# A graph network on one core: bfloat16 parts in attention's block products, and no counting of sources

## The chip, the core and the metric

The kernel runs on one core of one Trainium2 chip. A core has five engines with instruction streams of their own: PE (TensorE: matrix products; loading its weights is shown as PEld), DVE (VectorE), ACT (ScalarE), POOL (GpSimd) and SP (SyncE). They share the on-chip memory SBUF; products land in PSUM[...], which PE, DVE and ACT can reach. DMA queues, fed by SP, ACT and POOL, move data between SBUF and the chip's main memory. The metric is the device time of one execution in microseconds (us).

## The reference

There are 6,250 nodes with 128 features, 200,000 edges (source, destination, 16 attributes), the edges sorted by destination. Two blocks are added to the residual stream `x`:

```python
h = jnp.maximum(_layernorm(x, axis=-1), 0.0)
x = x + _L0_gnn_ref(h, edge_index, edge_attr_16, ...)     # five attention layers
h = jnp.maximum(_layernorm(x, axis=-1), 0.0)
x = x + _L1_gnn_ref(h, src, dst, theta_w, ...)            # edge convolution
```

An attention layer computes, for every edge and every self loop, a score, a softmax over the edges of one destination, and the weighted sum of the source rows:

```python
h = x @ W
s = leaky_relu((h @ a_src)[src] + (h @ a_dst)[dst] + (ea @ We) @ a_edge, 0.2)
ex = jnp.exp(s - segment_max(s, dst)[dst])
out = segment_sum(h[src] * (ex / denom[dst])[:, None], dst) + b
```

The edge convolution makes a row for each edge, normalizes each feature over all edges, multiplies, normalizes again and takes the mean over the edges of a destination:

```python
e = (h[dst] - h[src]) @ theta_w.T + h[src] @ phi_w.T
e = relu(_bn(e, bn0_g, bn0_b))      # mean and variance over the edges
e = relu(_bn(e @ fc1_w.T, bn1_g, bn1_b))
x = relu(segment_sum(e, dst) / maximum(count, 1) + h)
```

## The kernel before

**Tiling.** Nodes lie in 49 tiles of 128 (`NB`). The edges of a destination are cut into rows of K = 4 edges, padded; 128 such rows make a block, and four blocks (`GQ`) a group, so a group has 16 x 128 edge places. A loop `over` (L125) is written out for 109 groups; further groups for other inputs stand behind an `If` that this input doesn't enter. All rows of a block belong to one node tile. `neq` and `eqt` are the 0/1 matrices of a block (row by node of the tile) and are loaded from main memory group by group, in bfloat16.

**Stages, in order.**
1. *Sort and rows.* The degree of each destination is counted (`count`, L187): for 16 edges per partition at a time DVE makes two 0/1 arrays (L196, L198), and PE multiplies and adds them up (L200). From the degrees come the positions of the rows; POOL fetches the edge records (L480) and DVE makes the lists of indices `srci`.
2. *Five attention layers* (`attention`, L565). `heads` (L544) computes the node rows with their two scores and writes them to a table in main memory. Then come the groups, in `some` (L590). POOL issues 16 indirect DMAs (L594), each of which fetches 128 rows of the table into `g`; `g` has four buffers. DVE adds the scores (`t`, L605), finds each row's maximum and spreads it over the block (`z`, L611), PE transposes (L614), DVE takes the maximum and the running maximum (L615 to L629) and PE returns it to the rows (L636). After the exponential (L644), ACT makes the first of four weighted source rows (`yp`, L650), DVE adds the other three (L653), which gives `y`, 129 columns per row (features and a one for the denominator). ACT makes the 0/1 matrix `oh` in float32 (L656), PE adds the rows of each node, `op` = `oh` times `y` (L660), and DVE adds `op` into `hb` (L663), whose place for a block is read into a register.
3. Between layers: division, bias, a mix with the first layer's result and a small product, then the next `heads`.
4. *Edge convolution.* Node products `A` (for the destination) and `Bt` (for the source) are made; the mean over all edges is a product of the degrees with `A` and `Bt` (L771, L772) and is subtracted from `Bt`, so the sum of squares gives the variance. `A` is kept as three bfloat16 arrays whose sum is the float32 value (`A3`). The **first pass** (L790) gathers `Bt` rows, 16 indirect DMAs a group (L794), lets PE spread `A` over the rows (L804, three bfloat16 products per block, added in PSUM), adds the two (L808), transposes (L811), copies to `xs` (L812), sums squares on ACT (L814), and writes `xs` out. The second and third passes read these back and need no gather.

**Counting of sources.** The mean needs to know how often each node is a source, `outdeg`. It is counted in the attention layers, a fifth of the edges in each: `count` is a generator, and every fifth group asks for its next step (L665). In the compiled order many of these steps stand near the layer's start.

**Order.** Every engine works its own list in a fixed order; the framework draws it up from the program and adds the waits. It mixes operations of neighbouring groups: in attention, `t` of a group is placed ahead of L653 of the group two before it.

Of the kernel before, what the change touches and what calls it, by code (L numbers as in the profile page):

```python
# [9 lines left out]
F32 = mybir.dt.float32  # L10
BF = mybir.dt.bfloat16
I32 = mybir.dt.int32
AF = mybir.ActivationFunctionType
OP = mybir.AluOpType
AX = mybir.AxisListType
# [5 lines left out]
P = 128  # L21
K = 4
G = 16
GQ = G // K
# [7 lines left out]
def gnn_kernel(ctx: ExitStack, tc: tile.TileContext, x, src, dst, ea, Ws, Wes, a_srcs, a_dsts, a_edges,  # L32
# [8 lines left out]
    nc = tc.nc  # L41
    N, D = x.shape
# [49 lines left out]
    more = const.tile([1, 1], I32, name="more")  # L92
    outdeg = const.tile([P, NB], F32, name="outdeg")
    aeloop = const.tile([P, NB, L], F32, name="aeloop")
# [72 lines left out]
    with tc.tile_pool(name="gat", bufs=1) as gp:  # L167
# [14 lines left out]

        slo = gp.tile([P, CE], BF, name="slo")
        shi = gp.tile([P, CE], BF, name="shi")
        posb, vos, tb128, padq = adE, t0E, TS[:, 1:], R6[:, :, 0]

        def count(to, lo, hi, sw, pp, c0=0, c1=CE):  # L187

            po = pp.tile([P, 2, P], F32, name="po", bufs=1)

            io, po = po[:, 0, :], po[:, 1, :NB]
            nc.vector.tensor_copy(io, iota)
            for c in range(c0, c1, G):
                n = min(G, c1 - c)
                ol = sw.tile([P, G, P], BF, name="ol", bufs=2)
                nc.vector.tensor_tensor(ol[:, :n], mid_bc(io, n, P), last_bc(lo[:, c:c + n], n, P), OP.is_equal)  # L196
                oo = sw.tile([P, G, NB], BF, name="oo", bufs=2)
                nc.vector.tensor_tensor(oo[:, :n], mid_bc(io[:, :NB], n, NB), last_bc(hi[:, c:c + n], n, NB), OP.is_equal)  # L198
                for j in range(n):
                    nc.tensor.matmul(po, ol[:, j, :], oo[:, j, :], start=(c + j == c0), stop=(c + j == c1 - 1))  # L200
                yield
            nc.vector.tensor_tensor(to, to, po, OP.add)

# [18 lines left out]
        with tc.tile_pool(name="sort", bufs=1) as sp, tc.tile_pool(name="sortw", bufs=2) as sw, \  # L222
# [82 lines left out]
            halves(dsti, dlo, dhi)  # L305
            nc.vector.memset(deg, 0.0)
            nc.vector.memset(outdeg, 0.0)
            for _ in count(deg, dlo, dhi, sw, pp):
                pass
            halves(srcu, slo, shi)  # L310

# [253 lines left out]
        def attention(l):  # L565
# [20 lines left out]

            with tc.tile_pool(name="edg", bufs=2) as ep, tc.tile_pool(name="edgp", bufs=2, space=PSUM) as pp:
                steps = count(outdeg, slo, shi, ep, pp, CE * l // L, CE * (l + 1) // L)

                def some(q0, n):  # L590
# [54 lines left out]

                    y = ep.tile([P, GQ, D + 1], F32, name="y")
                    for h in range(0, GQ, 2):
                        yp = pp.tile([P, 2, D + 1], F32, name="yp", bufs=2)
                        for j in (h, h + 1):
                            nc.scalar.activation(yp[:, j - h, :], g[:, K * j, :D + 1], AF.Identity, bias=zeroc, scale=ex[:, j, 0:1])  # L650
                        for j in (h, h + 1):
                            for k in range(1, K):
                                nc.vector.scalar_tensor_tensor(y[:, j, :] if k == K - 1 else yp[:, j - h, :], g[:, K * j + k, :D + 1], ex[:, j, k:k + 1],  # L653
                                                               yp[:, j - h, :], op0=OP.mult, op1=OP.add)
                    oh = ep.tile([P, GQ, P], F32, name="oh")
                    nc.scalar.activation(oh, neq, AF.Identity, bias=onec, scale=-1.0)  # L656
                    for h in range(0, GQ, 2):
                        op = pp.tile([P, 2, D + 1], F32, name="op", bufs=2)
                        for j in (h, h + 1):
                            nc.tensor.matmul(op[:, j - h, :], oh[:, j, :], y[:, j, :], start=True, stop=True)  # L660
                        for j in (h, h + 1):
                            a = hbf[:, ds(r[j], D + 1)]
                            nc.vector.scalar_tensor_tensor(a, a, cor[:, j:j + 1], op[:, j - h, :], op0=OP.mult, op1=OP.add)  # L663

                    if q0 % (5 * GQ) == 0 and q0 < QM:  # L665
                        next(steps, None)

                over(GQ, some, lambda: nc.scalar.dma_start(ael[:, K * QM:], ae_d[l, :, K * QM:]))
                for _ in steps:
                    pass  # L670

# [61 lines left out]
    with tc.tile_pool(name="ec", bufs=1) as gp:  # L733
# [10 lines left out]
        nc.vector.memset(sc, 0.0)  # L744
        S0, SC0, S1, PAD, MU1, V1, SC1, SH1, T0, T1 = (sc[:, k:k + 1] for k in range(10))

        with tc.tile_pool(name="ecn", bufs=1) as lp, tc.tile_pool(name="ecp", bufs=2, space=PSUM) as pp:
# [13 lines left out]
            for t in range(0, NB, 2):  # L761
# [5 lines left out]
                nc.vector.tensor_copy(Bt[:, t:t + n, :], ps[:, :n, 1, :])  # L767

            mp = pp.tile([P, D], F32, name="mp", bufs=1)
            for t in range(NB):  # L770
                nc.tensor.matmul(mp, deg[:, t:t + 1].to_broadcast([P, P]), A[:, t, :], start=(t == 0), stop=False)  # L771
                nc.tensor.matmul(mp, outdeg[:, t:t + 1].to_broadcast([P, P]), Bt[:, t, :], start=False, stop=(t == NB - 1))  # L772
            mu = lp.tile([P, D], F32, name="mu")
# [11 lines left out]

        st0 = gp.tile([P, Q], F32, name="st0")
        with tc.tile_pool(name="p1", bufs=2) as ep, tc.tile_pool(name="p1p", bufs=4, space=PSUM) as pp:
            nc.vector.memset(st0, 0.0)

            def some(q0, n):  # L790
                c0 = K * q0
                g = ep.tile([P, G, D], F32, name="g1", bufs=4)
                for j in range(G):
                    nc.gpsimd.indirect_dma_start(  # L794
                        out=g[:, j, :], out_offset=None, in_=btable,
                        in_offset=bass.IndirectOffsetOnAxis(ap=srci[:, c0 + j:c0 + j + 1], axis=0))
                r = regs(3, q0, GQ, PE, (NB - 1) * 3 * P)
                eqt = ep.tile([P, GQ, P], BF, name="eqt1", bufs=4)
                nc.sync.dma_start(eqt, eqt_d[q0 // GQ])

                ar = pp.tile([P, GQ, D], F32, name="ar", bufs=2)
                for j in range(GQ):
                    for k in range(3):
                        nc.tensor.matmul(ar[:, j, :], eqt[:, j, :], A3f[:, ds(r[j] + k * D, D)], start=(k == 0), stop=(k == 2))  # L804
                xs = ep.tile([P, G, P], F32, name="xs", bufs=3)
                for j in range(GQ):
                    xe = ep.tile([P, K, D], F32, name="xe", bufs=4)
                    nc.vector.tensor_tensor(xe, g[:, K * j:K * j + K, :], mid_bc(ar[:, j, :], K, D), OP.add)  # L808
                    ps = pp.tile([P, K, P], F32, name="xps")
                    for k in range(K):  # L810
                        nc.tensor.transpose(ps[:, k, :], xe[:, k, :], ident)  # L811
                    nc.vector.tensor_copy(xs[:, K * j:K * j + K, :], ps)  # L812
                    sq = ep.tile([P, K, P], F32, name="sq")
                    nc.scalar.activation(sq, ps, AF.Square, accum_out=st0[:, q0 + j:q0 + j + 1])  # L814
                nc.sync.dma_start(e0_d[c0 // G], xs.rearrange("p a b -> p (a b)"))

            over(GQ, some)
        nc.vector.tensor_reduce(S0, st0, AX.X, OP.add)

# [5 lines left out]

        scale_of(SC0, S0, bn[:, 0:1])
        npad = float(C * P - E)


        with tc.tile_pool(name="p2", bufs=3) as ep, tc.tile_pool(name="p2p", bufs=4, space=PSUM) as pp:  # L830
            nc.vector.tensor_scalar(T1, bn[:, 1:2], 0.0, None, op0=OP.max)
            ps = pp.tile([P, 1], F32, name="padp", bufs=1)
# [8 lines left out]
            def some(q0, n):  # L841
                i = q0 // GQ
                xs = ep.tile([P, G * P], F32, name="x2")
                nc.sync.dma_start(xs, e0_d[i])
                nc.scalar.activation(xs, xs, AF.Relu, bias=bn[:, 1:2], scale=SC0)
                for q in range(G // 4):
                    ps = pp.tile([P, 512], F32, name="eps")
                    nc.tensor.matmul(ps, fT, xs[:, q * 512:(q + 1) * 512], start=True, stop=True)
                    k = (i * (G // 4) + q) * 2
                    nc.vector.bn_stats(st[:, k:k + 2, :].rearrange("p a b -> p (a b)"), ps)  # L850
# [38 lines left out]
        with tc.tile_pool(name="p4", bufs=3) as ep, tc.tile_pool(name="p4p", bufs=4, space=PSUM) as pp:  # L889
            def some(q0, n):  # L890
# [5 lines left out]
                nc.sync.dma_start(neq, neq_d[i])  # L896
                nc.scalar.activation(es, es, AF.Relu, bias=bn[:, 1:2], scale=SC0)
                oh = ep.tile([P, GQ, P], F32, name="oh4", bufs=2)
# [76 lines left out]
```

## Time and profile before

| | us |
|---|---|
| median of 3 runs (16198.5 to 16206.34) | 16200.36 |
| the profiled execution | 18742.08 |
| its span, first to last instruction | 18740.2 |
| first row gather of attention | 1379.1 |
| last gather of attention | 14792.8 |
| gathers of the first pass | 15025.6 to 17620.5 |

The profiled execution took longer than the timed runs, so its durations of single operations are of use, and its total isn't the total of the runs. In the tables "busy" is the time in which an engine worked, and "idle before" is the time for which it stood ahead of operations of a group, with what ended it. The mean granted TensorE clock was 0.537 of full speed.

In 40 slices of the span, busy tenths of three engines:

```profile
DVE  6433333334333343333343333433333422222378
ACT  0110111111111111111111111111111101111267
POOL 0555666646666646666646666556666356666300
```

The five layers and the first pass can be seen in POOL's row as the stretch from the third slice to the thirty-eighth, with a lower slice where a layer ends.

### The profile page before, as it was taken

Reading aid. Unit: us, or ns where it says so; the run is one execution under the profiler, and the core shown is the slowest. Engines: PE = TensorE matmul, PEld = TensorE weight load, DVE = VectorE, ACT = ScalarE, POOL = GpSimd, SP = SyncE. Lnnn points to the kernel's source line nnn. Section 1 sums busy time; section 2 is a strip of 40 time slices with the busy share of each in tenths; the row PEclk is TensorE's granted clock in tenths of the full one; section 3 lists DMA queues with packets and bytes.
Section 4 is the critical chain, followed back from the end, with each engine's and each line's share of the span. In section 5 each row is a group of like instructions: output and inputs, shape, how many; then the busy total and the mean of one; then the engine's idle time right before and its main releaser. Section 6 shows DMA issues by size and latency. Waiting matters only on the chain. (4 is left out here: it accounts for less than half of the span.)

```text
span 18740.2 us, 108293 instructions
## 1 busy us (share of the span) xinstructions
PE 4383.7 (23%) x24113; PEld 3257.3 (17%) x24113; DVE 7280.4 (39%) x23779; ACT 2812.4 (15%) x5544; POOL 10364.1 (55%) x10984
## 2 busy tenths in 40 slices
PE   4111111111111121111121111211111212222498
PEld 3111111111111111111111111111111111111268
DVE  6433333334333343333343333433333422222378
ACT  0110111111111111111111111111111101111267
POOL 0555666646666646666646666556666356666300
PEclk6555555555555555555555555555555555555699
DMA  3122222232222222222222222222222223333475
GB/s 100 41 60 50 57 55 57 58 60 54 57 57 56 57 55 57 58 57 58 56 55 57 57 57 56 56 57 57 57 58 56 62 87 93 95 95 92 145 254 201
DMA packets 717079, 1361.81 MB, mean 73 GB/s; under 512 B 223808, under 2 KB 486880, under 8 KB 673632
## 3 DMA queue, kind: packets, MB, share of 16 engines
q0 software_dynamic: 348800, 702.54, 18.3%
q1 hardware_dynamic: 338828, 616.20, 10.1%
q10 hardware_dynamic: 28756, 35.62, 0.6%
q8 instruction: 213, 3.49, 0.1%
q14 instruction: 482, 3.95, 0.1%
HBM read 1144.99 MB, written 208.56 MB: 72 GB/s over the span
## 5 line engine op out<-in xcount | busy, mean ns | idle before, releaser
L594 POOL DMA_INDIRECT g<-table,srci x8720 | 8229.2, 944 | 5241.1 <-issue 4659.1
L660 PE MATMUL op<-y,oh 128*128 128x129 f32 x4360 | 1455.5, 473 | 4624.1 <-DVE y L653 3021.3
L794 POOL DMA_INDIRECT g<-btable,srci x1744 | 1645.8, 944 | 1181.9 <-issue 512.7
L660 PEld LDWEIGHTS op<-y,oh 128*128 128x128 f32 x4360 | 1043.0, 318 | 5086.6 <-issue 3637.1
L653 DVE SCALAR_TENSOR_TENSOR yp<-g,ex,yp 128x129 f32<-128x129 f32 x4360 | 1331.7, 352 | 1393.6 <-DVE yp L653 735.5
L656 ACT ACTIVATE oh<-neq,onesq 128x512 f32<-128x512 bf16 x545 | 392.7, 721 | 5499.8 <-PE op L660 4182.0
L614 PE MATMUL xp<-ident,z 128*128 128x128 f32 x2180 | 607.4, 434 | 2482.5 <-issue 724.1
L663 DVE SCALAR_TENSOR_TENSOR hb<-hb,cor,op 128x129 f32 x2180 | 760.7, 349 | 981.7 <-PE op L660 421.0
L812 DVE COPY xs<-xps 128x512 f32<-128x512 f32 x436 | 301.6, 692 | 2068.2 <-remote 1358.8
L811 PE MATMUL xps<-ident,xe 128*128 128x128 f32 x1744 | 468.4, 423 | 2023.8 <-DVE xs L812 783.8
L653 DVE SCALAR_TENSOR_TENSOR y<-g,ex,yp 128x129 f32<-128x129 f32 x2180 | 693.5, 345 | 499.3 <-DVE y L653 278.2
L650 ACT ACTIVATE yp<-g,zeroc,ex 128x129 f32<-128x129 f32 x2180 | 880.0, 448 | 18.6
L480 POOL DMA_INDIRECT rg<-rec_d,rowi x436 | 472.1, 1083 | 672.4 <-DVE ix L473 371.2
L636 PE MATMUL mt<-R,eqt 128*128 128x6 bf16 x2180 | 135.4, 167 | 3010.5 <-DVE R L219 2333.4
L614 PEld LDWEIGHTS xp<-ident,z 128*128 128x128 f32 x2180 | 389.5, 217 | 2531.1 <-issue 735.0
L644 ACT ACTIVATE ex<-v 128x16 f32<-128x16 f32 x545 | 117.5, 216 | 4344.5 <-issue 1762.4
L615 DVE TENSOR_REDUCE tm<-xp 128x4 f32<-128x512 f32 x545 | 376.8, 691 | 977.6 <-issue 507.9
L811 PEld LDWEIGHTS xps<-ident,xe 128*128 128x128 f32 x1744 | 308.6, 215 | 2169.1 <-issue 2158.2
L636 PEld LDWEIGHTS <-eqt 128*128 128x128 bf16 x2180 | 104.9, 105 | 3151.2 <-issue 3151.0
L814 ACT ACTIVATE sq<-xps 128x512 f32<-128x512 f32 x436 | 260.3, 597 | 2393.3 <-DVE xs L812 1644.0
L611 DVE SCALAR_TENSOR_TENSOR z<-neq,mt 128x512 f32<-128x512 bf16 x545 | 374.6, 687 | 106.5 <-DVE t L605 56.1
L200 PE MATMUL po<-oo,ol 128*128 128x49 bf16 x3126 | 167.6, 217 | 1060.7 <-DVE oo L198 666.0
(317 smaller groups left out, 8606.8 us busy)
## 6 DMA issues: line engine op xcount, KB each, us to landing
g<-table,srci POOLq DMA_INDIRECT x8720
e_d<-xs SPq DMA_DIRECT2D x109, 1024.0 KB
x<-e_d SPq DMA_DIRECT2D x109, 1024.0 KB
e<-e_d SPq DMA_DIRECT2D x109, 1024.0 KB
neq<-neq_d SPq DMA_DIRECT2D x654, 128.0 KB
eqt<-eqt_d SPq DMA_DIRECT2D x654, 128.0 KB
g<-btable,srci POOLq DMA_INDIRECT x1744
table<-hb SPq DMA_DIRECT2D x5, 3185.0 KB
```

Source lines behind the costliest of these rows:

```text
L480: nc.gpsimd.indirect_dma_start(out=rg[:, j, :, :].rearrange("p k r -> p (k r)"), out_offset=None, in_=rec_d, in_offset=bass.IndirectOffset ...
L594: nc.gpsimd.indirect_dma_start(out=g[:, j, :], out_offset=None, in_=table, in_offset=bass.IndirectOffsetOnAxis(ap=srci[:, c0 + j:c0 + j + ...
L611: nc.vector.scalar_tensor_tensor(z, neq, -BIG, last_bc(tk, GQ, P), op0=OP.mult, op1=OP.add)
L614: nc.tensor.transpose(xp[:, j, :], z[:, j, :], ident)
L615: nc.vector.tensor_reduce(tm, xp, AX.X, OP.max)
L650: nc.scalar.activation(yp[:, j - h, :], g[:, K * j, :D + 1], AF.Identity, bias=zeroc, scale=ex[:, j, 0:1])
L653: nc.vector.scalar_tensor_tensor(y[:, j, :] if k == K - 1 else yp[:, j - h, :], g[:, K * j + k, :D + 1], ex[:, j, k:k + 1], yp[:, j - h, : ...
L656: nc.scalar.activation(oh, neq, AF.Identity, bias=onec, scale=-1.0)
L660: nc.tensor.matmul(op[:, j - h, :], oh[:, j, :], y[:, j, :], start=True, stop=True)
L663: nc.vector.scalar_tensor_tensor(a, a, cor[:, j:j + 1], op[:, j - h, :], op0=OP.mult, op1=OP.add)
L794: nc.gpsimd.indirect_dma_start(out=g[:, j, :], out_offset=None, in_=btable, in_offset=bass.IndirectOffsetOnAxis(ap=srci[:, c0 + j:c0 + j + ...
L811: nc.tensor.transpose(ps[:, k, :], xe[:, k, :], ident)
```

## The change

It has four parts, which the diff has together.

- In attention the sum `yp` is taken apart into three bfloat16 arrays: ACT copies it to bfloat16, DVE subtracts the copy, ACT copies the rest, DVE subtracts again. `oh` is bfloat16. One product per block gives all three parts side by side (3 x 129 columns), and DVE adds the parts (`tensor_reduce` into `sm`), then adds `sm` into `hb` as before. All three additions of L653 now stay in PSUM.
- `outdeg` and its counting go. For the mean, every node is taken as a source equally often (`E / N`).
- Since the mean is then only near the true one, the first pass also sums the values themselves, in the copy to `xs`, and the scale and a shift `SH0` are worked out from both sums.
- The first pass multiplies by the three parts of `A` side by side in one product per block, and DVE adds them.

```diff
@@ attention @@
-                steps = count(outdeg, slo, shi, ep, pp, CE * l // L, CE * (l + 1) // L)
...
-                    y = ep.tile([P, GQ, D + 1], F32, name="y")
+                    oh = ep.tile([P, GQ, P], BF, name="oh")
+                    nc.scalar.activation(oh, neq, AF.Identity, bias=onec, scale=-1.0)
+                    y3 = ep.tile([P, GQ, 3, D + 1], BF, name="y3")
                     for h in range(0, GQ, 2):
                         yp = pp.tile([P, 2, D + 1], F32, name="yp", bufs=2)
                         for j in (h, h + 1):
                             nc.scalar.activation(yp[:, j - h, :], g[:, K * j, :D + 1], AF.Identity, bias=zeroc, scale=ex[:, j, 0:1])
+                        for k in range(1, K):
+                            for j in (h, h + 1):
+                                nc.vector.scalar_tensor_tensor(yp[:, j - h, :], g[:, K * j + k, :D + 1], ex[:, j, k:k + 1],
+                                                               yp[:, j - h, :], op0=OP.mult, op1=OP.add)
+                        nc.scalar.copy(y3[:, h:h + 2, 0, :], yp)
+                        nc.vector.tensor_tensor(yp, yp, y3[:, h:h + 2, 0, :], OP.subtract)
+                        nc.scalar.copy(y3[:, h:h + 2, 1, :], yp)
+                        nc.vector.tensor_tensor(y3[:, h:h + 2, 2, :], yp, y3[:, h:h + 2, 1, :], OP.subtract)
...
+                        sm = pp.tile([P, 2, D + 1], F32, name="sm", bufs=1)
                         for j in (h, h + 1):
-                            nc.tensor.matmul(op[:, j - h, :], oh[:, j, :], y[:, j, :], start=True, stop=True)
+                            op = pp.tile([P, 3, D + 1], F32, name="op", bufs=2)
+                            nc.tensor.matmul(op, oh[:, j, :], y3[:, j], start=True, stop=True)
+                            nc.vector.tensor_reduce(sm[:, j - h, :], op.rearrange("p a d -> p d a"), AX.X, OP.add)
...
-                    if q0 % (5 * GQ) == 0 and q0 < QM:
-                        next(steps, None)
@@ mean over the edges @@
+            en = lp.tile([P, P], F32, name="en")
+            nc.vector.memset(en, float(E) / N)
...
-                nc.tensor.matmul(mp, outdeg[:, t:t + 1].to_broadcast([P, P]), Bt[:, t, :], start=False, stop=(t == NB - 1))
+                nc.tensor.matmul(mp, en, Bt[:, t, :], start=False, stop=(t == NB - 1))
@@ first pass @@
-                ar = pp.tile([P, GQ, D], F32, name="ar", bufs=2)
+                ar = pp.tile([P, GQ, D], F32, name="ar", bufs=1)
                 for j in range(GQ):
-                    for k in range(3):
-                        nc.tensor.matmul(ar[:, j, :], eqt[:, j, :], A3f[:, ds(r[j] + k * D, D)], start=(k == 0), stop=(k == 2))
+                    a3 = pp.tile([P, 3, D], F32, name="a3", bufs=3)
+                    nc.tensor.matmul(a3, eqt[:, j, :], A3f[:, ds(r[j], 3 * D)], start=True, stop=True)
+                    nc.vector.tensor_reduce(ar[:, j, :], a3.rearrange("p a d -> p d a"), AX.X, OP.add)
...
-                    nc.vector.tensor_copy(xs[:, K * j:K * j + K, :], ps)
+                    nc.vector.tensor_scalar(xs[:, K * j:K * j + K, :], ps, 1.0, 0.0, op0=OP.mult, op1=OP.add, accum_out=st0[:, 0, q0 + j:q0 + j + 1])
```

After the first pass two reductions over the groups and six operations on one column take the place of one reduction; the later passes use `SH0` in place of the second column of `bn`. In the sort stage `count` is a plain function, the split of the source indices into two halves (four operations on 1,563 columns) is gone, and with it the arrays `slo` and `shi`.

More of the change, by code (lines that the diff above doesn't have):

```diff
@@ L92, in gnn_kernel @@
     more = const.tile([1, 1], I32, name="more")
-    outdeg = const.tile([P, NB], F32, name="outdeg")
     aeloop = const.tile([P, NB, L], F32, name="aeloop")
@@ L181, in gnn_kernel, with count @@
         nc.scalar.dma_start(table[NP + 1:, :].rearrange("(t q) w -> q t w", q=P), mid_bc(zr, NB, HW))
-        slo = gp.tile([P, CE], BF, name="slo")
-        shi = gp.tile([P, CE], BF, name="shi")
         posb, vos, tb128, padq = adE, t0E, TS[:, 1:], R6[:, :, 0]
-        def count(to, lo, hi, sw, pp, c0=0, c1=CE):
+        def count(to, lo, hi, sw, pp):
             po = pp.tile([P, 2, P], F32, name="po", bufs=1)
@@ L192, in count @@
             nc.vector.tensor_copy(io, iota)
-            for c in range(c0, c1, G):
-                n = min(G, c1 - c)
+            for c in range(0, CE, G):
+                n = min(G, CE - c)
                 ol = sw.tile([P, G, P], BF, name="ol", bufs=2)
@@ L199, in count @@
                 for j in range(n):
-                    nc.tensor.matmul(po, ol[:, j, :], oo[:, j, :], start=(c + j == c0), stop=(c + j == c1 - 1))
-                yield
-            nc.vector.tensor_tensor(to, to, po, OP.add)
+                    nc.tensor.matmul(po, ol[:, j, :], oo[:, j, :], start=(c + j == 0), stop=(c + j == CE - 1))
+            nc.vector.tensor_copy(to, po)
         def first(lp, pp):
@@ L305, in gnn_kernel @@
             halves(dsti, dlo, dhi)
[L306 to L310, printed above, removed]
+            count(deg, dlo, dhi, sw, pp)
             nxf = sp.tile([P, 1], F32, name="nxf")
@@ L650, in some @@
                             nc.scalar.activation(yp[:, j - h, :], g[:, K * j, :D + 1], AF.Identity, bias=zeroc, scale=ex[:, j, 0:1])
-                        for j in (h, h + 1):
[L652 to L660, printed above, removed]
+                        for k in range(1, K):
+                            for j in (h, h + 1):
+                                nc.vector.scalar_tensor_tensor(yp[:, j - h, :], g[:, K * j + k, :D + 1], ex[:, j, k:k + 1],
+                                                               yp[:, j - h, :], op0=OP.mult, op1=OP.add)
@@ new lines, in some @@
+                        nc.scalar.copy(y3[:, h:h + 2, 0, :], yp)
+                        nc.vector.tensor_tensor(yp, yp, y3[:, h:h + 2, 0, :], OP.subtract)
+                        nc.scalar.copy(y3[:, h:h + 2, 1, :], yp)
+                        nc.vector.tensor_tensor(y3[:, h:h + 2, 2, :], yp, y3[:, h:h + 2, 1, :], OP.subtract)
+                    for h in range(0, GQ, 2):
+                        sm = pp.tile([P, 2, D + 1], F32, name="sm", bufs=1)
+                        for j in (h, h + 1):
+                            op = pp.tile([P, 3, D + 1], F32, name="op", bufs=2)
+                            nc.tensor.matmul(op, oh[:, j, :], y3[:, j], start=True, stop=True)
+                            nc.vector.tensor_reduce(sm[:, j - h, :], op.rearrange("p a d -> p d a"), AX.X, OP.add)
@@ L661, in some @@
                         for j in (h, h + 1):
                             a = hbf[:, ds(r[j], D + 1)]
-                            nc.vector.scalar_tensor_tensor(a, a, cor[:, j:j + 1], op[:, j - h, :], op0=OP.mult, op1=OP.add)
-                    if q0 % (5 * GQ) == 0 and q0 < QM:
-                        next(steps, None)
+                            nc.vector.scalar_tensor_tensor(a, a, cor[:, j:j + 1], sm[:, j - h, :], op0=OP.mult, op1=OP.add)
                 over(GQ, some, lambda: nc.scalar.dma_start(ael[:, K * QM:], ae_d[l, :, K * QM:]))
-                for _ in steps:
-                    pass
@@ L744, in gnn_kernel @@
         nc.vector.memset(sc, 0.0)
-        S0, SC0, S1, PAD, MU1, V1, SC1, SH1, T0, T1 = (sc[:, k:k + 1] for k in range(10))
+        S0, SC0, S1, PAD, MU1, V1, SC1, SH1, T0, T1, SH0 = (sc[:, k:k + 1] for k in range(11))
         with tc.tile_pool(name="ecn", bufs=1) as lp, tc.tile_pool(name="ecp", bufs=2, space=PSUM) as pp:
@@ L783, in gnn_kernel @@
             nc.sync.dma_start(btable[NP + 1:, :].rearrange("(t q) d -> q t d", q=P), Bt)
-        st0 = gp.tile([P, Q], F32, name="st0")
+        st0 = gp.tile([P, 2, Q], F32, name="st0")
         with tc.tile_pool(name="p1", bufs=2) as ep, tc.tile_pool(name="p1p", bufs=4, space=PSUM) as pp:
@@ L811, in some @@
                         nc.tensor.transpose(ps[:, k, :], xe[:, k, :], ident)
-                    nc.vector.tensor_copy(xs[:, K * j:K * j + K, :], ps)
+                    nc.vector.tensor_scalar(xs[:, K * j:K * j + K, :], ps, 1.0, 0.0, op0=OP.mult, op1=OP.add, accum_out=st0[:, 0, q0 + j:q0 + j + 1])
                     sq = ep.tile([P, K, P], F32, name="sq")
-                    nc.scalar.activation(sq, ps, AF.Square, accum_out=st0[:, q0 + j:q0 + j + 1])
+                    nc.scalar.activation(sq, ps, AF.Square, accum_out=st0[:, 1, q0 + j:q0 + j + 1])
                 nc.sync.dma_start(e0_d[c0 // G], xs.rearrange("p a b -> p (a b)"))
             over(GQ, some)
-        nc.vector.tensor_reduce(S0, st0, AX.X, OP.add)
+        nc.vector.tensor_reduce(S1, st0[:, 0, :], AX.X, OP.add)
+        nc.vector.tensor_reduce(S0, st0[:, 1, :], AX.X, OP.add)
+        nc.vector.tensor_scalar(T1, S1, 1.0 / E, None, op0=OP.mult)
+        nc.vector.tensor_tensor(T0, S1, T1, OP.mult)
+        nc.vector.tensor_tensor(S0, S0, T0, OP.subtract)
+        nc.vector.tensor_scalar(S0, S0, 0.0, None, op0=OP.max)
         def scale_of(to, s, gamma):
@@ L826, in gnn_kernel @@
         scale_of(SC0, S0, bn[:, 0:1])
+        nc.vector.tensor_tensor(T1, T1, SC0, OP.mult)
+        nc.vector.tensor_tensor(SH0, bn[:, 1:2], T1, OP.subtract)
         npad = float(C * P - E)
         with tc.tile_pool(name="p2", bufs=3) as ep, tc.tile_pool(name="p2p", bufs=4, space=PSUM) as pp:
-            nc.vector.tensor_scalar(T1, bn[:, 1:2], 0.0, None, op0=OP.max)
+            nc.vector.tensor_scalar(T1, SH0, 0.0, None, op0=OP.max)
             ps = pp.tile([P, 1], F32, name="padp", bufs=1)
@@ L844, in some @@
                 nc.sync.dma_start(xs, e0_d[i])
-                nc.scalar.activation(xs, xs, AF.Relu, bias=bn[:, 1:2], scale=SC0)
+                nc.scalar.activation(xs, xs, AF.Relu, bias=SH0, scale=SC0)
                 for q in range(G // 4):
@@ L896, in some @@
                 nc.sync.dma_start(neq, neq_d[i])
-                nc.scalar.activation(es, es, AF.Relu, bias=bn[:, 1:2], scale=SC0)
+                nc.scalar.activation(es, es, AF.Relu, bias=SH0, scale=SC0)
                 oh = ep.tile([P, GQ, P], F32, name="oh4", bufs=2)
```

## The prediction

> **What bounds the kernel now.** I read the busy table first, then the costliest groups, then the POOL row of the timeline stage by stage, and last the ends of the five attention layers, because the chain of waits on the page covers only the final DVE operations and says nothing of the rest.
>
> ```profile
> PE 4383.7 (23%) x24113; PEld 3257.3 (17%) x24113; DVE 7280.4 (39%) x23779; ACT 2812.4 (15%) x5544; POOL 10364.1 (55%) x10984
> ...
> L594 POOL DMA_INDIRECT g<-table,srci x8720 | 8229.2, 944 | 5241.1 <-issue 4659.1
> L660 PE MATMUL op<-y,oh 128*128 128x129 f32 x4360 | 1455.5, 473 | 4624.1 <-DVE y L653 3021.3
> ```
>
> POOL is the busiest engine at only 55%, but a row gather takes 0.944 us plus a steady 0.30 us before the next. The timeline shows them 1.25 us apart in every undisturbed stretch, so a group of 16 costs 20.0 us. Attention has 5 layers x 109 groups: 545 x 20.0 = 10,900 us; the first pass of the edge part has 109 more, 2,180 us. Together 13,080 us, 81% of the 16,200 us measured.
>
> The profiled execution is longer: span 18,740.2, time 18,742.1 us, 2,542 us over the median of the runs. In it the other engines sometimes stand still together:
>
> ```profile
> 4185.23 2.29 DVE L196 TENSOR_TENSOR ol<-po,slo 128x2048 bf16<-128x2048 f32 x1 [35.49 <-remote]
> ```
>
> After such a stall POOL finds no free g buffer. Of 540 strides between groups, 217 are 20.0 us and the rest longer. First to last gather takes 2,563 to 2,611 us a layer, 12,908 in all, against 5 x 2,178 without stalls (108 full strides and 16 gathers); the first pass takes 2,596. That is 2,018 + 418 = 2,436 us of stall, nearly the whole 2,542. So I take the timed runs to be at the gather pace, and count changes on the stages outside it. DVE and PE work beside the gathers is then free as long as buffers come back in time.
>
> A layer's end is not beside gathers. Layer 2:
>
> ```profile
> 9374.98 0.94 POOL L594 DMA_INDIRECT g<-table,srci  x1 [0.30 <-issue]
> 9376.23 0.94 POOL L594 DMA_INDIRECT g<-table,srci  x1 [0.30 <-issue]
> ...
> 9387.08 0.18 DVE L605 TENSOR_TENSOR t<-g,ael 128x16 f32<-128x16 f32 x1 [5.69 <-DMA g<-table,srci]
> ...
> 9413.12 1.58 DVE L663 SCALAR_TENSOR_TENSOR hb<-hb,cor,op 128x129 f32 x4 [0.63 <-PE op L660]
> ```
>
> L605 is the last group's first operation. After it DVE still works through three groups' L653 and L663, since its fixed order runs t two groups ahead of y. The table by stretches for this tail (us, then busy PE, PEld, DVE, ACT, POOL):
>
> ```profile
> 9387.08:9414.75 27.67, 10.01 (x40) 7.40 (x40) 20.74 (x87) 6.51 (x18) 0.00 (x0) 0.50 0.10 33
> ```
>
> The other four tails are 27.3 to 27.7 us with the same 20.6 to 20.7 us of DVE. Nothing else runs, POOL is at zero, and output, next table and next first gather wait for it. This is where added DVE work costs time.
>
> **The change, part by part.** *Attention's products.* Per group of four blocks PE loses eight f32 matmul instructions (473 ns each in the row above) and gets four bf16 ones of 387 columns. Beside gathers this is worth nothing: PE is 23% busy and waits for y. ACT gains four copies of 258 elements; the nearest row is the 256-element copy, 374 ns. DVE gains four subtractions of 258 and four reductions 387 to 129:
>
> ```profile
> L615 DVE TENSOR_REDUCE tm<-xp 128x4 f32<-128x512 f32 x545 | 376.8, 691 | 977.6 <-issue 507.9 <-PE xp L614 354.5 <-remote 115.2
> ...
> L531 DVE TENSOR_REDUCE s<-p 128x80 f32<-128x240 f32 x27 | 10.8, 401 | 122.0 <-remote 118.6 <-PE p L527 3.3
> ...
> L767 DVE COPY Bt<-abp 128x256 f32<-128x256 f32 x24 | 10.2, 425 | 22.5 <-ACT A L766 22.5
> L766 ACT COPY A<-abp 128x256 f32<-128x256 f32 x24 | 9.0, 374 | 13.7 <-PE abp L765 13.7
> ```
>
> Between 240 (401 ns, the same part-by-part reduction) and 512 elements (691 ns) a reduction of 387 is 558 ns; a subtraction I put at the 256-element copy's 425 ns. 4 x 0.42 + 4 x 0.56 = 3.92 us. The Trainium skill, VectorE: DVE Perf Modes, section "The DRAIN you can't avoid", says that the next operation doesn't start until the pipe is empty; that gives 3.92. The timeline shows four L653 of 0.35 us in 1.13 us, so successive windows overlap by about 0.08 us; eight operations then add 3.3 us. I take the row: 9.9 us for the three groups of a tail against 11.8 by the rule, or 50 against 59 us over five layers.
>
> Is it all added? The tail holds 6.8 us without DVE work (mean 27.5 - 20.7). In the first two groups new work can fall into such waits; I count 1 us each, as their waits for PE are 0.46 and 0.56 us. In the last group nothing fills, and the second half's two ACT copies (2 x 0.38, with their hand-overs 1.1 us) are exposed. 2 x 2.3 + 4.4 = **9.0 us a layer**, 45 in all. Bounds: all waits but a little filled, 4 us a layer; every copy of three groups exposed, 15.
>
> While gathers run, a free group takes 10.7 us from L663 to L663, hence some 14 with the change, under 20. Buffers: g has four, so gathers of group i+4 start 80 us after those of group i. Group i+2 has landed 60 + 1.9 us after that start (1.9 us is the lag from the last gather's end to L605 where DVE waits only for it), and L653 of group i ends 6 to 9 us later: 68 to 71 us. The new ACT and DVE work comes after those reads; even 3.3 us before them leaves 6.
>
> *Counting of sources.* About 20 steps a layer of 2.29 + 0.96 us of DVE go. Five stand ahead of the layer's first t, which waits 18 us for landing anyway; the others lie in the next eight or so groups, one or two in each (10.7 + 2 x 3.3 = 17.3 us, under 20). Worth 0, bounded below by the rival further on. In the sort stage four operations of 0.95 us and two memsets go; they stand between counting steps which wait 0.9 us for PE, so -1 us of at most -4.
>
> *First pass.* PE issues 4 products where it had 12. DVE gains four reductions, 384 to 128, about 0.56 us each, 2.2 us a group; the accumulating form of the xs copy reads the same 512 PSUM elements as the 692 ns copy, and its accumulator read is 0.08 us at L552.
>
> ```profile
> 17643.28 0.69 DVE L812 COPY xs<-xps 128x512 f32<-128x512 f32 x1 [1.27 <-PE xps L811]
> 17643.89 0.68 DVE L808 TENSOR_TENSOR xe<-g,ar 128x512 f32<-128x512 f32 x1
> ```
>
> A block takes 2.56 us here, a group 10.3, at most 12.5 after, under 20; the 1.27 us waits for PE can even hold the reductions. Tail +1 us (0 to 2.5). Then one more reduction of 476 elements (0.65 us) and six operations on a column (0.15 each) precede the second pass, +1.6 us, of which its first activation, waiting for x anyway, hides about half: +1. The mean's products keep their number.
>
> Sum: 45 - 1 + 1 + 1 = **+46 us**, that is 16,246 against the runs' 16,200. A change of under 0.2%, 32 us, can't be told from none here.
>
> **A rule against the change.** The Trainium skill, SBUF — State Buffer, section "Who interferes with whom", says that a DVE operation with two SBUF inputs shuts out a GpSimd instruction that reads SBUF. The row stage shows it:
>
> ```profile
> 1225.66 2.28 DVE L515 TENSOR_TENSOR oh<-iota,dl 128x2048 bf16<-128x2048 f32 x1
> ...
> 1226.49 2.27 POOL L480 DMA_INDIRECT rg<-rec_d,rowi  x1 [0.30 <-issue]
> ```
>
> If the four subtractions did that, 545 x 1.7 = 926 us would be added. But each has yp, in PSUM, as one input, like L653 and L663 now, and beside those:
>
> ```profile
> L594 POOL DMA_INDIRECT g<-table,srci x8720: 938/944/962, 1379.1 to 14792.8; - x199
> ```
>
> The longest of 8,720 gathers is 962 ns. I take zero.
>
> **Rivals.** *A shallower order* (18%): the instruction order is redrawn for the new program; if only two groups remain after the last landing, or the waits take nearly all the work, the tail is 27.5 - 10 + 2 x 3.3 = 24.1 us, or with the waits filled +4 a layer: with the +1 of the rest -16 to +21, 16,184 to 16,221. For it: 6.8 us of waits. Against: the longer chain of a group makes more gaps for later groups, not fewer.
>
> *Counting was not hidden* (9%, the faster side): with two count steps between L605 of group 2 and the last L653 of group 0 the first buffer is back at 71 + 6.6 = 78 us, just under 80; from the third step on POOL stalls, and by then half of each step costs time. Thirteen steps x 3.25 / 2 = 21 us a layer, 105 in all: 16,246 - 105 = 16,141. For it: the strides after the first three are 28.6 and 27.2 us in layers 1 to 4. Against: a 35 us stall stands ahead of them.
>
> *POOL or DVE starved* (11%): if L605 ran three groups ahead of y, a buffer would return after 80 + 1.9 + 6 us and each group take 28 us, +4,400; if hand-overs lift a group over 20 us, at 21 it is +545, 16,745. For it: four more hand-overs between ACT and DVE. Against: 6 us of room in both sums.
>
> **Chances.** Forecast 62%, its own range 16,215 to 16,285. Slower by over 0.2% is most of it and the starved case: 0.68; the same: 0.23; faster, mostly the counting: 0.09. From 16,170 to 16,325 leaves out the counting case and the starved one.
>
> **What would show it.** Right: gathers still 1.25 us apart, 0.94 each; tails from the last L605 to the last addition into hb near 36 us, three groups in each; reductions near 0.56 us, subtractions 0.42; no count. Wrong: tails of 31 or less, strides over 20 us where DVE is not stalled, or a gather over 1 us in attention.

## The result, and the profile after

| | us |
|---|---|
| before, median of 14 runs (16196.1 to 16208.41) | 16200.58 |
| after, median of 14 runs (16225.7 to 16244.33) | 16236.34 |
| ratio after / before, 95% interval | 1.0021 [1.0013, 1.0029] |
| profiled execution of after: time, span | 16238.29, 16236.5 |

The change makes the kernel 35.8 us slower, 0.22%. The profiled execution of after took as long as its timed runs, unlike that of before, so here the stages can be read directly. In all later runs, on two chips, the kernel before took about 18,680 to 18,850 us, like its first profile and unlike the runs in this table. I call this the **paced** condition and that of the table the **quiet** one; what tells them apart is shown below.

The page of after, its busy table, POOL's row in 40 slices, and five groups:

```profile
span 16236.5 us, 105136 instructions
...
PE 3831.9 (24%) x19498; PEld 2228.9 (14%) x19498; DVE 8539.8 (53%) x28803; ACT 3562.8 (22%) x7724; POOL 10364.1 (64%) x10984
...
POOL 0466777757777757777757777577777377777200
...
L584 POOL DMA_INDIRECT g<-table,srci x8720 | 8227.6, 944 | 3229.6 <-issue 2597.9
...
L595 DVE TENSOR_TENSOR t<-g,ael 128x16 f32<-128x16 f32 x545 | 99.0, 182 | 4944.1 <-DMA g<-table,srci 4898.4
...
L657 DVE TENSOR_REDUCE sm<-op 128x129 f32<-128x387 f32 x2180 | 1232.5, 565 | 43.5 <-DVE R L215 1.6
...
L651 DVE TENSOR_TENSOR y<-yp,y 128x258 bf16<-128x258 f32 x1090 | 451.1, 423 | 15.3
L649 DVE TENSOR_TENSOR yp<-yp,y 128x258 f32<-128x258 f32 x1090 | 433.4, 430 | 22.0 <-ACT y L648 0.9
```

DVE has 5,024 more instructions and still waits at every group for its rows: 4,898 us in 538 waits, 9.1 us each. DVE's timeline shows this as a clock of 20 us:

```profile
8366.88 0.18 DVE L595 TENSOR_TENSOR t<-g,ael 128x16 f32<-128x16 f32 x1 [9.12 <-DMA g<-table,srci]
...
8386.87 0.18 DVE L595 TENSOR_TENSOR t<-g,ael 128x16 f32<-128x16 f32 x1 [8.92 <-DMA g<-table,srci]
...
8406.81 0.18 DVE L595 TENSOR_TENSOR t<-g,ael 128x16 f32<-128x16 f32 x1 [8.02 <-DMA g<-table,srci]
```

None of the 648 strides between groups, in five layers and the first pass, is over 20.1 us. First to last gather takes 2,176.5 to 2,176.8 us in each layer and 2,176.6 in the first pass. So nothing of the added work beside the gathers is paid here. The layers' tails, from the last `t` to the last addition into `hb`, are 35.16, 35.16, 35.18, 35.26 and 34.30 us, where before has 27.27, 27.33, 27.62, 27.27 and 27.63: 37.9 us more in all. The third tail in the table by stretches (us; busy time of PE, PEld, DVE, ACT, POOL with instructions; clock, DMA share, GB/s), and its end in DVE's timeline:

```profile
8118.41:8153.59 35.18, 6.87 (x24) 2.11 (x24) 30.99 (x112) 10.53 (x29) 0.00 (x0) 0.50 0.08 27
```

```profile
8147.55 0.77 DVE L649 TENSOR_TENSOR yp<-yp,y 128x258 f32<-128x258 f32 x2 [0.18 <-ACT y L648]
8148.43 0.76 DVE L651 TENSOR_TENSOR y<-yp,y 128x258 bf16<-128x258 f32 x2
8149.46 1.24 DVE L657 TENSOR_REDUCE sm<-op 128x129 f32<-128x387 f32 x2 [0.27 <-PE op L656]
```

DVE's work in it rose from 20.74 to 30.99 us, the time without DVE work fell from 6.9 to 4.2. The tails give +37.9 us where the runs give +35.8; the rest of the change together is then -2.1 us. The kernel before was never profiled in the quiet condition, so its tails here are those of its paced profile. The tails of after are alike in both (175.0 us in all here, 175.4 paced).

### The profile page after: what moved, and what is told of

It reads as the page before. It is cut to its first block, busy times and chain, and to the rows that moved or that the text cites. A ratio compares the mean times of both kernels' runs of the same rounds, so it can differ in the third digit from the quotient of the medians.

```text
span 16236.5 us, 105136 instructions
## 1 busy us (share of the span) xinstructions
PE 3831.9 (24%) x19498; PEld 2228.9 (14%) x19498; DVE 8539.8 (53%) x28803; ACT 3562.8 (22%) x7724; POOL 10364.1 (64%) x10984
## 5 line engine op out<-in xcount | busy, mean ns | idle before, releaser
L656 PE MATMUL op<-y,oh 128*128 128x387 bf16 x2180 | 988.8, 506 | 7825.7 <-DVE y L651 7503.3
L645 DVE SCALAR_TENSOR_TENSOR yp<-g,ex,yp 128x129 f32<-128x129 f32 x6540 | 1787.8, 351 | 13.9 <-ACT yp L642 13.6
L648 ACT CAST y<-yp 128x258 bf16<-128x258 f32 x1090 | 370.6, 377 | 5940.7 <-DVE yp L645 5940.7
L657 DVE TENSOR_REDUCE sm<-op 128x129 f32<-128x387 f32 x2180 | 1232.5, 565 | 43.5 <-DVE R L215 1.6
L803 DVE TENSOR_TENSOR xe<-g,ar 128x512 f32<-128x512 f32 x436 | 299.9, 688 | 1162.6 <-DMA g<-btable,srci 1162.2
L660 DVE SCALAR_TENSOR_TENSOR hb<-hb,cor,sm 128x129 f32 x2180 | 755.3, 346 | 65.0 <-DVE am L628 55.9
L637 ACT ACTIVATE oh<-neq,onesq 128x512 bf16<-128x512 bf16 x545 | 392.5, 721 | 888.0 <-PE op L656 809.0
L651 DVE TENSOR_TENSOR y<-yp,y 128x258 bf16<-128x258 f32 x1090 | 451.1, 423 | 15.3
L649 DVE TENSOR_TENSOR yp<-yp,y 128x258 f32<-128x258 f32 x1090 | 433.4, 430 | 22.0 <-ACT y L648 0.9
L650 ACT CAST y<-yp 128x258 bf16<-128x258 f32 x1090 | 393.7, 377 | 190.7 <-DVE yp L649 190.7
L907 PE MATMUL rps<-fs,e 128*128 128x128 f32 x3488 | 408.6, 276 | 4.6 <-ACT e L900 4.6
```

What stands on the lines that cost most here:

```text
L645: nc.vector.scalar_tensor_tensor(yp[:, j - h, :], g[:, K * j + k, :D + 1], ex[:, j, k:k + 1], yp[:, j - h, :], op0=OP.mult, op1=OP.add)
L649: nc.vector.tensor_tensor(yp, yp, y3[:, h:h + 2, 0, :], OP.subtract)
L651: nc.vector.tensor_tensor(y3[:, h:h + 2, 2, :], yp, y3[:, h:h + 2, 1, :], OP.subtract)
L656: nc.tensor.matmul(op, oh[:, j, :], y3[:, j], start=True, stop=True)
L657: nc.vector.tensor_reduce(sm[:, j - h, :], op.rearrange("p a d -> p d a"), AX.X, OP.add)
L660: nc.vector.scalar_tensor_tensor(a, a, cor[:, j:j + 1], sm[:, j - h, :], op0=OP.mult, op1=OP.add)
```

## The experiments

All runs are in the paced condition, and each ratio is against the kernel before, run on the same chip at the same time. There were four such times, at which the kernel before took 18,848 us (rows 1 to 4), 18,719 (rows 5 to 8), 18,690 (row 9) and 18,682 (rows 10 to 12). "Gathers" is the sum over five layers of first to last gather; "tail" is that of the third layer. The diffs below are shortened to what each edit does.

Two things limit comparisons between rows. An edit has the order of instructions drawn up anew: of 540 groups, DVE's order is that of after in 539 where only the last three groups are edited (rows 4 and 6), and that of before in 487 where the products are undone (rows 2 and 3); the other edits have orders of their own. And the pace was slower at the first time: before's unchanged first pass took 2,752 us then and 2,603 at the second (row 8), after's took 2,535 and 2,536 then (rows 2 and 4) and 2,492 to 2,505 at the later times.

| kernel | median | ratio [95%] | gathers | tail |
|---|---|---|---|---|
| before, again | 18850.38 | one run | 12,884 | 27.63 |
| attention's products undone | 18479.94 | 0.9795 [0.9781, 0.9808] | 12,731 | 27.43 |
| and the first pass's too | 18739.31 | 0.9936 [0.9922, 0.9949] | 12,719 | 27.42 |
| old products in the last three groups | 19136.91 | 1.0153 [1.0140, 1.0167] | 13,390 | 25.51 |
| reductions tripled in the middle | 20139.44 | 1.0761 [1.0746, 1.0775] | 14,331 | 35.34 |
| reductions tripled in the tails | 18936.78 | 1.0118 [1.0103, 1.0133] | 13,127 | 45.93 |
| after, two groups left | 19141.12 | 1.0231 [1.0217, 1.0246] | 13,370 | 23.22 |
| before, two groups left | 19048.25 | 1.0182 [1.0166, 1.0198] | 13,264 | 16.91 |
| products undone, fewer left | 18186.56 | 0.9733 [0.9720, 0.9747] | 12,495 | 14.28 |
| after, again | 18877.66 | 1.0100 [1.0086, 1.0113] | 13,146 | 35.17 |
| parts added in PSUM | 18429.85 | 0.9858 [0.9843, 0.9874] | 12,722 | 30.51 |
| after, fewer left | 19505.68 | 1.0435 [1.0421, 1.0449] | 13,770 | 21.30 |

### Before and after again: what the paced condition is

> The kernel before, unchanged, for a profile of it. Theory (the gather pace holds everywhere outside the stages): if this execution has no stalls, its span is near 16,200 us, the strides between groups are 20.0 us in all five layers, a layer's gathers take 2,177 us, and the tails from the last t to the last addition into hb are 27.3 to 27.6 us. Rival (counting of sources is not hidden): strides of over 20 us near the start of each layer, where the counting steps stand, about 21 us a layer in sum.

> The kernel after, unchanged, beside the kernel before on this call's chip. If the kernel before takes 16,200 us here: 16,236 us, ratio 1.002. If it takes 18,690 to 18,850 us, as in the three calls so far: the tails are 35 us and the gather stages those of the kernel with more reductions in the tails alone (2,610 to 2,666 us in the layers, 2,505 in the first pass), so 18,937 - 5 x 10.9 = 18,880 us, ratio 1.008 to 1.010: added DVE work is then paid beside the gathers as well. Rival (in that condition too only the tails count): 36 us more than before.

Before, again: the condition "no stalls" didn't come about; 297 of its 540 strides in attention are over 20.1 us. After, again: 18,877.66 us where 18,880 was expected. Its all-engine timeline in the middle of a layer, with the gathers left out, shows what is different:

```profile
8008.45 0.35 DVE L660 SCALAR_TENSOR_TENSOR hb<-hb,cor,sm 128x129 f32 x1 [1.14 <-DVE mt L598]
...
8009.15 0.17 DVE L631 SCALAR_TENSOR_TENSOR v<-v 128x16 f32<-128x16 f32 x1 [0.35 <-DVE hb L660]
...
8010.55 0.69 DVE L601 SCALAR_TENSOR_TENSOR z<-neq,mt 128x512 f32<-128x512 bf16 x1 [1.23 <-DVE v L631]
...
8011.95 0.57 DVE L657 TENSOR_REDUCE sm<-op 128x129 f32<-128x387 f32 x1 [0.71 <-DVE z L601]
...
8013.35 0.17 DVE L632 TENSOR_TENSOR v<-v,am 128x16 f32<-128x16 f32 x1 [0.83 <-DVE sm L657]
...
8014.77 1.12 PE L604 MATMUL xp<-ident,z 128*128 128x128 f32 x4 [8.60 <-DVE t L595]
```

The operations take as long as ever (the reduction 0.57 us), but one that waits for another often starts 0.70 or 1.40 us after the last start. PE is late as well: its product at 8014.77 starts 3.5 us after the end of `z`, which it reads. Between first and last gather of attention, 1,321 of 23,974 starts of DVE in this trace lie 1.375 to 1.425 us after the one before; in the first trace of after none of 23,983 does. All but one of the 1,321 lie within the layers' gathers, not between them.

The pace doesn't simply follow POOL. In this window POOL stands still from 8023.5 to 8031.3 us; DVE is paced until about 8029, and then runs at full speed until 8043.9 although the gathers go on. In the first pass the hand-overs from engine to engine are later still. At the place below PE's product ends at 15383.87, and the DVE copy that reads it starts 8.7 us later, with DVE idle in between:

```profile
15382.79 1.08 PE L806 MATMUL xps<-ident,xe 128*128 128x128 f32 x4 [26.77 <-issue]
...
15392.55 0.69 DVE L807 TENSOR_SCALAR_CACHE_REDUCE xs<-xps 128x512 f32<-128x512 f32 x1 [9.90 <-remote]
```

The granted clock doesn't tell the conditions apart: 0.538 to 0.576 in the quiet runs of after, 0.533 to 0.567 in its paced ones.

With these late starts DVE falls behind and returns `g` late, as the list of waits of the two traces of after shows (us in total, times, longest), first the quiet one:

```profile
DVE t L595 <- DMA g<-table,srci: 4898.4, 538, 35.8
```

```profile
POOL g L584 <- ACT y L648: 1759.6, 187, 15.9
...
POOL g L584 <- ACT y L650: 563.5, 74, 9.6
```

In the quiet trace DVE waits for POOL; in the paced one POOL waits for a buffer that the late weighted sums still hold (L648 and L650 are the next ACT operations in that chain). Here added work beside the gathers is paid: the gathers take 13,146 us against 12,884 and 12,908 in the two traces of before.

### The parts of the change, one by one

```diff
-  y3 (three bf16 parts), op 3 x 129, tensor_reduce into sm
+  y (f32), op = oh (f32) times y, as before           # products undone
...
-  a3 = eqt times A3 (3 x 128); tensor_reduce into ar
+  three products per block, added in PSUM             # first pass's too
```

> The kernel after, with attention's products as before (one float32 product per block, y in SBUF, no parts and no reductions). The counting stays out, the first pass stays new. Theory (the added work costs only in the five tails, 7 to 8 us each): about 36 to 38 us less than after, 16,200 us, tails back at 27.3 us. Rival (attention's parts cost elsewhere, or the rest of the change costs): more than half of the +36 us stays, 16,218 us or more. Rival (the counting was not hidden in the kernel before, and its removal gave back a part of what the products cost): clearly under before, 16,150 us or less.

> The kernel after, with attention's products as before and also the first pass's products as before (three per block, added in PSUM). What stays of the change is that nothing is counted and that the statistics are made from both sums. Theory (counting lay beside the gathers): 16,198 to 16,202 us, as before. Rival (counting was not hidden): 16,150 us or less. First pass: its new products are worth the difference to the kernel with attention's products alone undone, expected 0 to 2 us.

The expected times were for the quiet condition; paced, the stages separate the parts.

- *Not counting, with the new statistics*: ratio 0.9936, 110 to 120 us gained. The layers' gathers fall by 165 us and the first pass, with its new sums, grows by 56. The place fits: the first twelve strides of layers 2 to 4 take 309 to 310 us in before again and 278 to 281 without counting.
- *The first pass's one product*: 18,739 to 18,480, 259 us gained, with a first pass of 2,535 us in place of 2,808. This is at the slower first time; at the second time the new first pass, its sums included, was only 98 to 111 us shorter than the old one.
- *Attention's parts*: undone and not undone ran at different times, so their cost is rough. The gathers differ by 415 us (12,731 to 13,146), and the time from last gather to the next stage's first by 49 us in all (722 to 770.5): some 460 us lost, the new order of instructions included.

So paced, counting was *not* hidden, and the parts cost far more than their tails. Undoing the parts brings the tails back to 27.3 to 28.0 us, as expected.

### Where added DVE work is paid

```diff
+  if QM - 3 * GQ <= q0 < QM:   # old f32 products here, parts elsewhere
...
-  tensor_reduce(sm, op)
+  for _ in range(3 if q0 < QM - 6 * GQ else 1): tensor_reduce(sm, op)           # middle
...
+  for _ in range(3 if QM - 3 * GQ <= q0 < QM else 1): tensor_reduce(sm, op)     # tails
```

> The kernel after, but the last three groups of each layer use the old float32 product; the other 106 groups of a layer keep the parts, copies, subtractions and reductions. Theory (the cost lies in the tails alone): 36 us less than after, near 16,200 us, tails near 27.4 us, though 97% of the added work is still there. Rival (the cost is spread over all groups): 16,235 us, as after, with at most 1 us gained.

> The kernel after, with each reduction of op to sm issued three times instead of once in all groups of a layer but the last six: eight more reductions, about 4 us of DVE, in each of 103 groups, 515 groups in all, some 2,000 us of DVE work. The sums are the same. Theory (work beside gathers is free as long as a group stays under 20 us): 16,236 us, as after, within 5 us. Rival (added DVE work is paid wherever it stands): up to 16,236 + 2,000 us; a tenth of it would be 16,440.

> The kernel after, with each reduction of op to sm issued three times in the last three groups of each layer alone: 24 more reductions a layer, 120 in all, at about 0.48 us behind one another. Theory (a tail pays nearly all of it): 24 x 0.48 = 11.5 us a layer, 58 us, 16,290 us, tails near 46 us. If half of it falls into waits: 16,265. Rival (tails have room): no change, 16,236.

**Tails.** Here the theory holds: tails hold no gathers, and after's read alike in both conditions. The third tails, first with the reductions tripled there, then with the old products there:

```profile
9542.65:9588.58 45.93, 7.19 (x24) 2.29 (x24) 42.89 (x136) 10.41 (x29) 0.00 (x0) 0.50 0.06 21
```

```profile
9655.48:9680.99 25.51, 9.23 (x36) 6.84 (x36) 20.87 (x88) 6.33 (x17) 0.00 (x0) 0.50 0.11 37
```

24 more reductions lengthen this tail by 10.8 us over after's 35.17, 0.45 us each (0.48 expected). From last gather to the next stage's first, summed over the layers, they add 61 us (832 against 770.5). With the old products in three groups alone the tail falls by 9.7 us, below before's, and this sum by 44 us (726). Tripling in the middle leaves the tails at 34.5 to 35.7.

**Beside the gathers.** Here the theory fails in the paced condition. 4,120 reductions in the middle lengthen the gathers by 1,186 us, 0.29 us each. Between the theory's 0 and the rival's 0.48 that is closer to the rival. The kernel with old products in the last three groups was expected 36 us under after and came out above it, 1.0153 against 1.0100: its gathers take 244 us more, 1.9%, though DVE's order in its middle groups is the same. It ran at the slower first time, when the first pass, which it has in common with after, took 1.7% more (2,536 against 2,494 us). Steps of 1.42 to 1.43 us between DVE's starts are 164 in its trace, 10 in that of after again. So a slower pace is the likely reason; a run of after at that time, which would show it, is missing.

### Which added work makes the tail

```diff
-  tensor_reduce(sm[:, j - h, :], op, add)     # one product per block, 3 x 129
+  three products per block into op[:, j - h, :], start / stop; op goes into hb
```

> The kernel after, but the three parts are added in PSUM (three bfloat16 products per block with start and stop) and op is added into hb directly: no reductions, 12 products a group instead of 4. The copies and subtractions stay. Theory (the tail is DVE's work for three groups): 4 x (0.565 - 0.08) = 1.9 us less of DVE in each group, 5.8 us a tail at most; tails of 29.5 to 31 us where after has 35.2, so the reductions are some two thirds of the change's cost. If the hand-overs of the copies are what costs instead: tails of 34 to 35. In time 20 to 28 us less than after on a chip at 16,200.

```profile
9252.99:9283.50 30.51, 8.79 (x52) 5.50 (x52) 24.93 (x99) 10.67 (x30) 0.00 (x0) 0.50 0.10 31
```

Without reductions the tail is 30.51 us: of the 7.7 us between 27.43 and 35.17, the reductions make 4.7, copies and subtractions 3.1. In this condition the kernel is 448 us faster than after, 424 of it in the gathers. Eight more products a group on PE weigh less than four reductions on DVE in the tail; of the 424 us, the share of the reductions isn't separated from that of the order, which also changed (`z` now stands right behind `t`, as in before). It also beats before here; in the quiet condition, where only the 5 x 4.7 us of tails could be gained, I'd estimate 16,213 us, which was not run.

### Fewer groups left at the end

```diff
-  t = ep.tile([P, GQ, K], F32, name="t")
+  t = ep.tile([P, GQ, K], F32, name="t", bufs=1)             # two groups left
...
+  tx = ep.tile([P, 2, GQ, K], F32, name="tx", bufs=1)
+  t, ex = tx[:, 0], tx[:, 1]                                  # fewer left
```

> The kernel after with one buffer for t instead of two. The instruction order is drawn up anew, and t of a group then stands one group ahead of the weighted sums instead of two, so two groups' sums are left after the last t instead of three. Theory (the tail is the number of groups left times what a group takes): one group of 11 to 13 us less in each tail, 24 us, 16,175 us. Rival (what sets the end is when the last rows land, and the number of groups left does not matter): 16,236. Danger: a group's chain has less cover; strides over 20 us would show it.

> The kernel before with one buffer for t instead of two: two groups left after the last t instead of three. Theory: 9 to 10 us less in each tail, about 18 us, 16,152 us. Rival: 16,200, as before. If both this and the same edit of the kernel after gain by their own group time, the cost of the change is the groups left times the added time of one, so the change costs about 25 us here instead of 36.

> The kernel after with attention's products as before (one float32 product per block), so no parts are made, and with t and ex in one tile of one buffer: the order is drawn up anew, and t of a group then follows all twelve weighted additions of the group before it, so two groups' block products and one group's weighted sums are left after the last t. Theory (a tail is the number of groups left times the time of one): tails of 13 to 17 us instead of 27.3. On a chip on which the kernel before takes 16,200 us, that gives 5 x 10 to 14 us less: 16,130 to 16,150. On a chip on which the kernel before takes 18,700 to 18,850 (as in the two calls so far, where DVE's operations start 0.70 or 1.40 us apart while gathers run), the tails are the same 13 to 17 us, but a chain with one group of cover makes the gather stages longer than those of the kernel with only the products undone: 18,600 to 19,100. Rival (the tail is set by the landing of the last rows, not by the groups left): tails of 27 us.

> The kernel after with t and ex in one tile of one buffer, so that t of a group follows the weighted additions of the group before it; products in parts as in after. Theory (tail is the groups left times the time of one): tails of 18 to 22 us instead of 35.2; by the tails alone 65 to 85 us less than after. Rival: tails of 35. In the gather stages a group's chain is near 20 us here, so these may be longer than after's.

The tail follows the number of groups left: a group less takes off 12.0 us in after and 10.7 in before; with still fewer left it is 14.28 us with the products undone and 21.30 in after. But a shorter tail isn't an earlier end. Paced, DVE is behind when the last gather is issued. With the products undone, the last `t` came 8.7 to 10.0 us after the last gather's end in the deep order and 21.3 to 30.1 in the shallow one, and the sum from last gather to next first gather didn't fall (722 and 736 us). In the quiet condition, where DVE waits for the rows at each `t`, it should fall; that is argued, not shown. In the gathers the shallower order lost in three kernels (224 to 624 us). The fourth, with the products undone, was expected at 18,600 to 19,100 us and took 18,186.56, with gathers 236 us shorter than in the deep order. But the deep one ran at the slower first time, and 236 us is 1.9%, about that difference, so a gain from the shallower order isn't shown; that it didn't lose here stays unexplained. At 0.9733 this kernel is the shortest of all here and beats both kernels.

## Why the prediction was right, and where it wasn't

**Right, in the condition of the runs.** Forecast 16,246, measured 16,236.34, by the mechanism named: in the quiet trace of after, gathers at 20.0 us a group everywhere and the whole cost in the tails. That the 2,436 us of stalls in the first profile were not in the timed runs of before is inferred from their time of 16,200 us, as no quiet trace of before exists. Durations were close: reduction 565 ns (558 forecast), subtractions 423 and 430 (425), copies 377 (374).

**The mis-sized term** is the tail, 9.0 us forecast, 7.6 measured on average (37.9 / 5). In the third layer the added DVE work was nearly right: 20.74 to 30.99 is 10.25 us, where the row of overlapping operations gave 9.9 and the rule of the empty pipe 11.8. Too low was what falls into waits: 2 us forecast, 2.7 measured. And most of the 1.1 us of copies exposed in the last group isn't there: L649 waits 0.18 us for its copy.

**The small terms.** Sort, first pass and statistics were +1 together; what is left is -2.1. That the counting was worth about 0 in the quiet condition follows from this sum: the rival's saving of 105 us would need further costs of 103 us, and the trace of after, with every stride at 20.0 us, has no place for them. No quiet run isolates it.

**The port rule.** Taken as zero, and so it was; the form of the gathers in the quiet trace of after (ns, least, median, longest):

```profile
L584 POOL DMA_INDIRECT g<-table,srci x8720: 938/944/987, 1330.1 to 12732.9; - x199
```

The longest took 987 ns; no subtraction shut a gather out.

**What was incomplete** is the step from the extra 2,542 us to stalls of that one execution, which I set aside as nothing to do with the change. It was a condition that held in all later runs, at four times and on two chips, and in it the change costs 1.0%, not 0.2%. The sentence "DVE and PE work beside the gathers is then free as long as buffers come back in time" has the right proviso: paced, they don't. The starved rival named this end (strides over 20 us) but by longer hand-overs of the new kernel, not by a pace that both kernels share. The before-profile showed it: only 217 of 540 strides at 20.0 was a sign that work beside the gathers was already paid there. Had the timed runs been of this kind, the forecast would have been some 150 us short.

## What to carry to other kernels

Find the wait that shows slack (here 9.1 us per group at the first operation on gathered rows): while it is there, added work on that engine is free beside the gathers and paid only in the drain behind the last one, at the groups still outstanding times the added time of each. When a profile disagrees with the timed runs, work the change out for both: the same edit can be free in one and cost a per cent in the other. And where PE has room, adding parts up in PSUM can cost less than a reduction on the vector engine that drains the stage (tails of 30.5 us against 35.2). Lastly, where the pace of a chip drifts, two kernels are compared only when both ran at the same time.

## What the runs showed of the hardware

- While a layer's gathers run, waiting operations on DVE can start 0.70 or 1.40 us apart, in some executions and not in others; PE started 3.5 us after the operation that it waited for at one place, and DVE 8.7 us after PE in the first pass. All this comes with unchanged durations (gathers 943 and 944 ns, reductions 566 and 565). It cost the kernel before some 2,500 us. That PE is held too speaks against a port between DVE and POOL as the only cause. What makes the pace stays open.
- In the quiet trace of after, `t` starts on a group's rows mostly 1.7 to 2.2 us after its last gather when more gathers follow, but 8.8 to 10.4 us after it when none do (8118.41 against 8109.35 in the third layer). This is some 7 us at each layer's end, which no kernel here tried to take away.
